# Attention scores on the two halves of TensorE: two of four query tiles with their halves swapped, and GpSimd's three steps on q and k in another order

## The chip, the cores and the metric

The kernel runs on one core of a Trainium2 chip. The metric is the device time of one execution in microseconds, the median of several runs. All work is in float32, on the core's five engines: TensorE (PE in the profile; PEld is its weight load), VectorE (DVE), ScalarE (ACT), GpSimd (POOL) and SyncE (SP), which issues the DMAs.

## The reference, cut to what matters

Four layers, each `x = x + layernorm(layer(layernorm(x)))`, on x of 2 batches x 512 tokens x 256 features. Only the first, causal attention with rotary positions, is touched by the change:

```python
q = rope((x @ wq.T + bq).reshape(b, s, 16, 128))
k = rope((x @ wk.T + bk).reshape(b, s, 16, 128))
v = (x @ wv.T + bv).reshape(b, s, 16, 128)
attn = einsum('bihd,bjhd->bhij', q, k) / sqrt(128)
attn = softmax(where(j > i, -inf, attn), axis=-1)
return einsum('bhij,bjhd->bihd', attn, v).reshape(b, s, 2048) @ wo.T + bo + residual
```

with `rope(x) = x * cos + rotate_half(x) * sin`. The other three are a feed-forward layer whose weights are unpacked from 4-bit codes (hidden size 2048, GELU), a linear attention with running sums, and a feed-forward layer whose weights are looked up in a table of 16 values (hidden size 688, SiLU).

## The kernel before, in words

**Tiles and halves.** A token tile is P = 128 tokens, so a batch has NT = 4 of them; HALF is 64. Once `halved[0]` is set, `matmul` (line 280) issues each matmul of 128 output rows as two of 64: the first writes PSUM partitions 0 to 63, the second 64 to 127. In the profile such a matmul has the form 128*64, and the two run on different column halves of the array. The text calls them A and B. A float32 matmul stands in the profile as two passes, each with its own weight load.

**Slots.** Attention is a loop over 32 heads (16 for each of 2 batches). `slot(i)` writes, in program order for each engine:

- the scores of head i, for the query tiles in the order 3, 2, 0, 1. Tile `it` sees (it+1) x 128 keys. `score_matmul` gives each half only the keys that its 64 queries may see: half A stops 64 keys before half B, and the 64 columns that A leaves out are filled with zeros by a small bf16 matmul (line 937), so that VectorE reads no stale PSUM. Tiles 2 and 0 share a PSUM bank; tile 1 lies in a bank of the tag "t".
- `scores` on VectorE: scores plus a causal mask, into the SBUF tile `p`, with a running minimum of the negated result; `exps` on ScalarE: the exponentials and their sums.
- `project` for q, then for k, of head i+1: four matmuls of 512 columns (two halves x two chunks of 128 features), then the rotary product. For k, ScalarE makes `ra` (k plus bias), GpSimd multiplies it by cosines; for q, VectorE makes bias, sum and product in one operation. VectorE makes two operations `rr` for the rotated part by sines. GpSimd adds `ra` and `rr` to qT or kT (for k of heads 0 and 1 VectorE does). In GpSimd's queue this stands as: q's sum, k's product by cosines, k's sum.
- the output projection of head i-2 (`projected_out`), accumulated over the heads of a batch in two PSUM banks; `attended` for head i-1 (probabilities by values: for key tile jt the 512 - 128 jt queries that see it); the transposed probabilities of head i (`turned_p`: VectorE's block transposes, then four DMAs to pT); one quarter of v for the group two ahead (`values`).

Head i+1's first score matmul needs qT and kT whole. Between the steps a slot also issues work for later layers: `dequantised` unpacks 4-bit weights (every second slot), `look_up` writes terms of a table look-up (VectorE makes a term, GpSimd adds it), and `vector.fill` puts steps of a selection wherever a planner in the file (`Times`, `Engine`, `now`, `until`, `poll`) expects VectorE to be free. The planner decides only the order of the program; nothing of it runs on the chip.

**Around it.** After the heads of a batch `after_attention` runs `norms` for units 0 and 1, or 2 and 3 (a unit is two token tiles); its last step is `yield until(to)`, which holds the chain back, in the planner's time, until its DMAs have landed. The first feed-forward layer begins inside the last slots (`next(main)`).

Of the kernel before, what the change touches and what calls it, by code (L numbers as in the profile page):

```python
# [10 lines left out]
F32 = mybir.dt.float32  # L11
I32 = mybir.dt.int32
# [7 lines left out]
P = 128  # L20
# [19 lines left out]
EPS = 1e-5  # L40
EPS_LIN = 1e-9
NEG = -1e30
WARM = 9
REST = INTER - (NO - 1) * P

# [144 lines left out]
def sandwich_kernel(  # L190
# [100 lines left out]
    def until(*aps):  # L291

        return max(0.0, times.written(*aps) - now[0])
# [30 lines left out]
    ident = const.tile([P, P], F32, name="ident")  # L324
    make_identity(nc, ident)

    mask = const.tile([P, S], F32, name="mask")

    def half(t, u):

        return t[:, HT * (u % 2) : HT * (u % 2) + HT, :]
# [26 lines left out]
    def norms(u, y, stage, to, eps=EPS, strided=False):  # L358

        x = [xs[u][:, j, :] for j in range(HT)]
        first = [stats(t, eps) for t in y]
        second = []
        for j in range(HT):
            yield until(first[j][0])
            add_scaled(x[j], y[j], first[j][0])
            second.append(stats(x[j], EPS))
        n = acts.tile([P, HT, D], F32, tag="ln", name=f"ln{stage}_{u}")


        by_blocks = (u, stage) != (NUNIT - 1, 3)
        for j in range(HT):
            rstd, shift = second[j]
            yield until(rstd, shift)
            to_n, from_x = n[:, j, :], x[j]
            if not by_blocks:
                to_n = to_n.rearrange("p (k f c) -> p k f c", k=NK, c=4)
                from_x = from_x.rearrange(
                    "p (c f k) -> p k f c" if strided else "p (k c f) -> p k f c", k=NK, c=4  # L380
                )
            elif strided:
                to_n = to_n.rearrange("p (k m) -> p k m", k=NK)
                from_x = from_x.rearrange("p (m k) -> p k m", k=NK)
            scalar.activation(to_n, from_x, AF.Identity, bias=shift, scale=rstd)
        yield until(n)
        if by_blocks:

            tr = acts.tile([P, 4, NK, HT, 32], F32, tag="ln", name=f"tr{stage}_{u}")
            for j in range(HT):  # L390
                vector.transpose(
                    tr[:, :, :, j, :], n[:, j, :].rearrange("p (k c f) -> p c k f", k=NK, c=4)
                )
            for a in range(4):
                sync.dma_start(
                    out=to[:, a].rearrange("p k j t -> p (k j t)"),
                    in_=tr[32 * a : 32 * a + 32].rearrange("f c k j t -> f c (k j t)"),
                )
        else:

            halved[0] = False
            pt = bank("t")
            for kc in range(NK):
                for j in range(HT):
                    transpose(
                        pt[:, kc * TU + j * P : kc * TU + (j + 1) * P],
                        n[:, j, kc * P : (kc + 1) * P],
                    )
            for kc in range(NK):
                scalar.copy(  # L410
                    to[:, :, kc].rearrange("p a j t -> p j a t"),
                    pt[:, kc * TU : (kc + 1) * TU].rearrange("p (j a t) -> p j a t", j=HT, a=4),
                )
        for j in range(HT):
            scalar.activation(x[j], x[j], AF.Identity, bias=first[j][1])
        yield until(to)


    terms = deque()
# [90 lines left out]
    with ExitStack() as at:  # L510
# [43 lines left out]
        def warm_up(n):  # L554
# [9 lines left out]
        xT0 = [  # L564
            ac.tile([P, NK, S] if b == 0 else [P, 4, NK, NT, 32], F32, name=f"xT0_{b}") for b in range(B)
        ]
        acc = ac.tile([P, NT, D], F32, name="h")


# [185 lines left out]
        def dequantised(packed, scales, u, name, w):  # L755
# [20 lines left out]
                    )  # L776
            p8 = dq.tile([P, UNIT], U8, tag="p8", name="p8")
            c8 = dq.tile([P, 2, UNIT], U8, tag="c8", name="c8")
            t8 = dq.tile([P, UNIT], U8, tag="t8", name="t8")
            two, t = p8.bitcast(I32), t8.bitcast(I32)  # L780
            low, high = c8[:, 0, :].bitcast(I32), c8[:, 1, :].bitcast(I32)

            def bits():
# [54 lines left out]

        def projection(kind, i, tag="mm"):

            b, h = divmod(i, NH)
            gg, hh = divmod(i, HG)
            w = wts[kind, gg]
# [6 lines left out]
            for cs in [slice(0, TU), slice(TU, S)] if i == 0 else [slice(0, S)]:  # L850
# [27 lines left out]
                )  # L878
                if first_half:
                    by_scalar()  # L880
            if (kind, i) == ("k", 1):
                inverted(0)
            (pool if i > 1 or kind == "q" else vector).tensor_add(to, a, r)
# [2 lines left out]
        def values(gg, pair, tag="mm"):  # L886
# [15 lines left out]
                    )  # L902
            scalar.copy(vs[gg][:, 2 * pair : 2 * pair + 2, :].rearrange("p t d -> p (t d)"), ps)

        def scores(i, it, ps):

            p, mn = ps_p[i]
            n = (it + 1) * P
            vector.tensor_tensor_reduce(
                out=p[:, p_at[it] : p_at[it] + n],  # L910
                in0=ps,
                in1=mask[:, S - n :],
                scale=-scale,
                scalar=3e38,
                op0=ALU.add,
                op1=ALU.min,
                accum_out=mn[:, it : it + 1],
            )


        zeros = mask[:, : HALF // 2].bitcast(mybir.dt.bfloat16)

        def score_matmul(i, it, ps):


            for q0 in (0, HALF):
                n = it * P + q0 + HALF
                matmul(
                    ps[q0 : q0 + HALF, :n],
                    qT[i][:, n - HALF : n],  # L930
                    kT[i][:, :n],
                    True,
                    True,
                    beside=q0 == 0,
                )
                if q0 == 0:
                    nc.tensor.matmul(  # L937
                        ps[:HALF, n : n + HALF], lhsT=zeros, rhs=zeros, start=True, stop=True
                    )

        def exps(i, it):
            p, mn = ps_p[i]
# [43 lines left out]
        def projected_out(i):  # L986

            b, h = divmod(i, NH)
            gg, hh = divmod(i, HG)
            if h == 0:  # L990
                yb[b] = [bank("o") for _ in range(NT // 2)]
            for t in range(NT):

                matmul(
                    yb[b][t // 2][:, (t % 2) * D : (t % 2 + 1) * D],
                    oT[i][:, t * P : (t + 1) * P],
                    wts["o", gg][:, hh, :],
                    h == 0 and t % 2 == 0,
                    h == NH - 1,
                    skip_group_check=True,  # L1000
                )

        def attention_sums(b):
            for t2 in range(NT // 2):
# [70 lines left out]
        def slot(i):  # L1075
# [29 lines left out]
            if now_in:  # L1105
                ps_p[i] = (
                    pr.tile([P, 1280], F32, tag="p", name="p"),
                    small.tile([P, NT], F32, tag="mn", name="mn"),
                )
                sums[i] = small.tile([P, NT], F32, tag="sm", name="sm")  # L1110
                s3 = bank("s")
                score_matmul(i, 3, s3)
                scores(i, 3, s3)
                s2 = bank("s")
                score_matmul(i, 2, s2[:, :384])
                score_matmul(i, 0, s2[:, 384:])
                scores(i, 2, s2[:, :384])
                exps(i, 3)
                scores(i, 0, s2[:, 384:])
                s1 = bank("t")  # L1120
                score_matmul(i, 1, s1[:, :256])
                scores(i, 1, s1[:, :256])
                exps(i, 2)
                exps(i, 0)
                exps(i, 1)
            catch_up()
            if i < NS - 2:
                look_up(i > 0)
            else:
                assert not terms  # L1130
            for kind in "qk":
                if kind == "q" and i in (0, 2, 3):
                    pass
                elif i + 1 < NS:
                    project(kind, i + 1)
                elif i <= NS:
                    next(main)
                    next(main)
                if kind == "q" and jobs and i % 2 == 0 and i >= 2:
                    dequantised(*jobs.popleft())  # L1140
                if kind == "q" and i and now_in:
                    inverted(i)
            if now_in:
                p, _ = ps_p[i]
                for it in reversed(range(NT)):
                    pi = p[:, p_at[it] : p_at[it] + (it + 1) * P]
                    scalar.mul(pi, pi, rs[i][:, it : it + 1])
# [14 lines left out]
            if now_in:  # L1162
                turned_p(i)
            if i in (1, 2):
                next(ahead, None)
            poll()
            if i < NS - HG:
                if i > 1:
# [9 lines left out]
        pair = projection("q", 0), projection("k", 0, "o")  # L1178
        next(pair[0])
        begin(first, next(first))  # L1180
        pool.affine_select(
            out=mask,
            in_=mask,
            compare_op=ALU.is_ge,
            fill=NEG,
            base=S - P,
            pattern=[[-1, S]],
            channel_multiplier=1,
        )
        halved[0] = True  # L1190
        next(pair[1])
        for step in (*pair, *pair):
            next(step, None)
        values(0, 0, "t")
        project("q", 1, "o")
# [318 lines left out]
```

## Time and profile before

| | |
|---|---|
| median of 3 runs | 626.18 us (626.04 to 626.4) |
| the profiled execution | 626.09 us, of which the span from the first to the last instruction is 624.3 us |
| TensorE | 617.4 us busy (99%), 4998 matmul records; granted clock 0.998 |
| VectorE | 487.9 us busy (78%) |
| ScalarE, GpSimd | 299.8 us (48%), 277.9 us (45%) |
| attention's slots | from 14.6 us to about 370 us |

A row of the profile's groups reads: line, engine, operation, output tile <- input tiles, shape, count, then busy time, mean ns of one and idle time ahead of it. A timeline row begins with its start and its length in us. A matmul's length runs to the modelled end of its pipeline, so that one begins before the end of the one ahead of it on the same half.

### The profile page before, as it was taken

Reading aid. Unit: us, or ns where it says so; the run is one execution under the profiler, and the core shown is the slowest. Engines: PE = TensorE matmul, PEld = TensorE weight load, DVE = VectorE, ACT = ScalarE, POOL = GpSimd, SP = SyncE. Lnnn points to the kernel's source line nnn. Section 1 sums busy time; section 2 is a strip of 40 time slices with the busy share of each in tenths; the row PEclk is TensorE's granted clock in tenths of the full one; section 3 lists DMA queues with packets and bytes.
Section 4 is the critical chain, followed back from the end, with each engine's and each line's share of the span. In section 5 each row is a group of like instructions: output and inputs, shape, how many; then the busy total and the mean of one; then the engine's idle time right before and its main releaser. Section 6 shows DMA issues by size and latency. Waiting matters only on the chain.

```text
span 624.3 us, 13250 instructions
## 1 busy us (share of the span) xinstructions
PE 617.4 (99%) x4998; PEld 443.5 (71%) x4998; DVE 487.9 (78%) x1159; ACT 299.8 (48%) x659; POOL 277.9 (45%) x351
## 2 busy tenths in 40 slices
PE   8999999999999999999999999999999999999996
PEld 6667766666676675677677789999766666666676
DVE  6979989877987989999998988779985372384853
ACT  5646666566565556656555751232213404416130
POOL 5355657355453465675667400450260151163341
PEclk9999999999999999999999999999999999999999
DMA  7467474575546646557462421311001001001000
GB/s 227 134 166 210 104 198 123 132 203 137 148 139 166 167 113 178 161 121 190 108 153 60 102 53 56 104 36 32 1 10 26 1 3 35 1 2 35 27 27 17
DMA packets 43600, 60.90 MB, mean 98 GB/s; under 512 B 5137, under 2 KB 31505, under 8 KB 43537
## 3 DMA queue, kind: packets, MB, share of 16 engines
q1 hardware_dynamic: 43536, 60.07, 36.9%
q8 instruction: 39, 0.64, 0.4%
q14 instruction: 25, 0.20, 0.1%
HBM read 28.33 MB, written 1.05 MB: 47 GB/s over the span
## 4 chain that ended last, share of the span: by engine, by line
PE 98%; issue 0%; DVE 0%; DMA 0%; POOL 0%; ACT 0%; POOLq 0%
PE ps_mm L280 40%; PE ps_o L280 22%; PE ps_s L280 21%; PE ps_t L280 15%; DMA x<-in_x 0%; DVE st L182 0%; PE ps_s L937 0%; POOLq L1510 0%; PE ps_t L287 0%; DVE mv L182 0%; POOL rstd L182 0%; ACT xT L182 0%; DVE x L182 0%; PE ps_s L287 0%; ACT wu L182 0%
## 5 line engine op out<-in xcount | busy, mean ns | idle before, releaser
L182 DVE SCALAR_TENSOR_TENSOR rr<-ps_mm,cols_sb,sin_sb 64x512 f32<-64x512 f32 (+1 forms) x126 | 93.4, 741 | 3.6 <-PE ps_mm L280 0.8
L182 POOL TENSOR_TENSOR wg<-wg,scratch 128x752 f32<-128x752 f32 x30 | 53.9, 1797 | 90.1 <-DVE scratch L182 87.4
L280 PE MATMUL ps_t<-pT,v 128*64 128x128 f32 (+3 forms) x512 | 88.6, 433 | 0.0
L280 PE MATMUL ps_mm<-xT,wg 128*64 128x256 f32 (+2 forms) x680 | 88.0, 379 | 0.0
L280 PE MATMUL ps_s<-xT,wu 128*64 128x256 f32 (+1 forms) x652 | 84.1, 379 | 0.0
L182 ACT ACTIVATE p<-p,mn 128x512 f32<-128x512 f32 (+3 forms) x128 | 70.6, 553 | 27.4 <-DVE mn L182 27.2
L280 PE MATMUL ps_o<-wd,hT 128*64 128x256 f32 (+2 forms) x676 | 78.4, 375 | 0.0
L280 PEld LDWEIGHTS ps_t<-pT,v 128*64 128x64 f32 x512 | 58.9, 137 | 23.8 <-issue 7.4
L280 PE MATMUL ps_o<-wo,oT 128*64 128x256 f32 x512 | 75.3, 379 | 0.0
L280 PE MATMUL ps_mm<-xT,wq 128*64 128x512 f32 (+2 forms) x252 | 73.9, 587 | 0.4 <-ACT xT L182 0.4
L280 PE MATMUL ps_mm<-xT,wk 128*64 128x512 f32 x248 | 73.2, 592 | 0.0
L280 PEld LDWEIGHTS ps_mm<-xT,wg 128*64 128x64 f32 (+2 forms) x680 | 59.5, 139 | 17.3 <-ACT ge L182 0.3
L280 PE MATMUL ps_s<-kT,qT 128*64 128x320 f32 (+5 forms) x384 | 71.5, 431 | 0.0
L280 PEld LDWEIGHTS ps_o<-wd,hT 128*64 128x64 f32 (+1 forms) x676 | 56.6, 141 | 19.6
L280 PEld LDWEIGHTS ps_s<-xT,wu 128*64 128x64 f32 (+1 forms) x652 | 57.6, 139 | 16.3 <-DVE hT L182 0.3
L280 PE MATMUL ps_mm<-wv,xTv 128*64 128x256 f32 x464 | 68.3, 379 | 0.0
L280 PEld LDWEIGHTS ps_o<-wo,oT 128*64 128x64 f32 x512 | 53.0, 137 | 19.9 <-issue 6.9
L182 ACT ACTIVATE p<-p,rs 128x512 f32<-128x512 f32 (+3 forms) x128 | 61.5, 551 | 10.1 <-DVE rs L182 8.2
L182 DVE CUSTOM_DVE_ANT_0 p<-ps_s,mask 128x512 f32<-128x512 f32 (+2 forms) x96 | 45.9, 509 | 25.6 <-PE ps_s L280 25.4
L182 POOL TENSOR_TENSOR qT<-ra,rr 128x512 f32<-128x512 f32 x32 | 40.9, 1277 | 47.9 <-DVE rr L182 47.9
L182 DVE STREAM_TRANSPOSE turned<-p 128x512 f32<-128x512 f32 (+3 forms) x128 | 54.1, 480 | 2.0 <-ACT p L182 1.1
L182 DVE TENSOR_TENSOR hT<-ge,ps_s 128x512 f32<-128x512 f32 x32 | 21.8, 683 | 41.4 <-ACT ge L182 22.9
(150 smaller groups left out, 992.5 us busy)
## 6 DMA issues: line engine op xcount, KB each, us to landing
pT<-turned SPq DMA_DIRECT2D x128, 208.0 KB, 3.9
wo<-in_wo SPq DMA_DIRECT2D x17, 256.0 KB, 4.0
wv<-in_wv SPq DMA_DIRECT2D x16, 256.0 KB, 4.0
wq<-in_wq SPq DMA_DIRECT2D x15, 256.0 KB, 4.7
wk<-in_wk SPq DMA_DIRECT2D x15, 256.0 KB, 4.5
xT<-tr SPq DMA_DIRECT2D x44, 64.0 KB, 2.2
pk_g<-in_gate_p SPq DMA_DIRECT2D x4, 256.0 KB, 4.2
sc_g<-in_gate_s SPq DMA_DIRECT2D x8, 128.0 KB, 4.1
```

What stands on the lines that cost most here:

```text
L182: return write(*args, **more)
L280: nc.tensor.matmul(out[part], lhsT=lhsT[:, part], rhs=rhs, start=start, stop=stop, **more)
```

## The change

1. `SWAPPED = (1, 2)`: in query tiles 1 and 2, the later 64 queries go to half A and the earlier 64 to half B. `score_matmul` becomes `score_half(i, it, late, ps)`, which issues one half of one tile, and `no_scores`, the zero fill. The order of issue becomes 3 early (A), 3 late (B), fill (A); 2 late (A), 2 early (B), 0 early (A), 0 late (B); 1 late (A), fill (B), 1 early (B). Tiles 2 and 0 lie in their shared bank so that each covers what the other leaves out, and need no fill.
2. The rows of `p` and the columns of pT and oT then stand in swapped order for tiles 1 and 2. `projected_out` puts them back: for each tile it issues the two halves itself, and sends each to the half where its tokens belong. In tiles 1 and 2 it issues B ahead of A.
3. The mask gets 128 columns more (the triangle for swapped tiles), moves to another SBUF pool, and is made by three selections of 128 columns instead of one of 512. `scores` reads it, the PSUM bank and `p` as blocks of 128 (64 for tile 0).
4. `projection` yields once more ahead of its sum. A slot first writes everything else of q and of k, and then the two sums. GpSimd's queue becomes: k's product by cosines, q's sum, k's sum. The dequantisation and the reciprocal `inverted(i)`, which stand between, are written ahead of both sums.
5. `dequantised` has no scratch tile `t8` of its own; it uses the first quarter of `pk`, the codes that it has read.
6. `norms` of unit 2 after attention ends with `yield 0.0` in the place of `yield until(to)`.

```diff
+SWAPPED = (1, 2)
-    mask = const.tile([P, S], F32, name="mask")
-        yield until(to)
+        yield 0.0 if (u, stage) == (2, 1) else until(to)
+        mask = ac.tile([P, S + P], F32, name="mask")
-            t8 = dq.tile([P, UNIT], U8, tag="t8", name="t8")
-            two, t = p8.bitcast(I32), t8.bitcast(I32)
+            two, t = p8.bitcast(I32), pk[:, : UNIT // 4]
...
+            yield
             if (kind, i) == ("k", 1):
                 inverted(0)
             (pool if i > 1 or kind == "q" else vector).tensor_add(to, a, r)
...
+        def score_half(i, it, late, ps):
+            n = it * P + (1 + late) * HALF
+            at = HALF * (late ^ (it in SWAPPED))
+            matmul(
+                ps[at : at + HALF],
+                qT[i][:, n - HALF : n],
+                blocks(kT[i][:, :n], HALF),
+                True,
+                True,
+                beside=not late,
+            )
...
+        def no_scores(ps):
+            nc.tensor.matmul(ps, lhsT=zeros, rhs=zeros, start=True, stop=True)
...
+                for half_ in range(2):
+                    at = HALF * (half_ ^ (t in SWAPPED))
+                    matmul(
+                        yb[b][t // 2][at : at + HALF, (t % 2) * D : (t % 2 + 1) * D],
+                        oT[i][:, t * P + half_ * HALF : t * P + (half_ + 1) * HALF],
+                        wts["o", gg][:, hh, :],
...
-                score_matmul(i, 3, s3)
-                scores(i, 3, s3)
+                score_half(i, 3, 0, blocks(s3[:, : S - HALF], HALF))
+                score_half(i, 3, 1, blocks(s3, HALF))
+                no_scores(s3[:HALF, S - HALF :])
+                scores(i, 3, blocks(s3, P))
                 s2 = bank("s")
-                score_matmul(i, 2, s2[:, :384])
-                score_matmul(i, 0, s2[:, 384:])
+                ps2 = s2[:, HALF : HALF + 3 * P]
+                ps0 = blocks(s2, P)[:, 0:4:3, :HALF]
+                score_half(i, 2, 1, blocks(ps2, HALF))
+                score_half(i, 2, 0, blocks(ps2[:, : 2 * P + HALF], HALF))
+                score_half(i, 0, 0, ps0[:, :1])
+                score_half(i, 0, 1, ps0)
...
-                score_matmul(i, 1, s1[:, :256])
-                scores(i, 1, s1[:, :256])
+                score_half(i, 1, 1, blocks(s1[:, :TU], HALF))
+                no_scores(s1[HALF:, TU - HALF : TU])
+                score_half(i, 1, 0, blocks(s1[:, : TU - HALF], HALF))
+                scores(i, 1, blocks(s1[:, :TU], P))
...
+            turning = []
             for kind in "qk":
...
-                    project(kind, i + 1)
+                    turning.append(projection(kind, i + 1))
+                    next(turning[-1])
+                    next(turning[-1])
...
+            for work in turning:
+                next(work, None)
```

More of the change, by code (lines that the diff above doesn't have):

```diff
@@ L903, in values, with blocks @@
             scalar.copy(vs[gg][:, 2 * pair : 2 * pair + 2, :].rearrange("p t d -> p (t d)"), ps)
+        def blocks(t, n):
+            return t.rearrange("p (b c) -> p b c", c=n)
         def scores(i, it, ps):
             p, mn = ps_p[i]
-            n = (it + 1) * P
+            n = HALF if it == 0 else P
+            masks = blocks(mask, P)
+            masks = (
+                blocks(mask[:, S - P : S], n),
+                masks[:, 0 : NT + 1 : NT],
+                masks[:, 0 : NT + 1 : NT // 2],
+                masks[:, :NT],
+            )
             vector.tensor_tensor_reduce(
-                out=p[:, p_at[it] : p_at[it] + n],
+                out=blocks(p[:, p_at[it] : p_at[it] + (it + 1) * P], n),
                 in0=ps,
-                in1=mask[:, S - n :],
+                in1=masks[it],
                 scale=-scale,
@@ L918, in scores @@
             )
-        zeros = mask[:, : HALF // 2].bitcast(mybir.dt.bfloat16)
[L923 to L939, printed above, removed]
+        def score_half(i, it, late, ps):
[8 more added lines that the diff above has]
+                beside=not late,
+            )
+        zeros = mask[:, : HALF // 2].bitcast(mybir.dt.bfloat16)
+        def no_scores(ps):
+            nc.tensor.matmul(ps, lhsT=zeros, rhs=zeros, start=True, stop=True)
         def exps(i, it):
@@ L992, in projected_out @@
             for t in range(NT):
[L994 to L1001, printed above, removed]
+                for half_ in range(2):
[4 more added lines that the diff above has]
+                        wts["o", gg][:, hh, :],
+                        h == 0 and t % 2 == 0,
+                        h == NH - 1,
+                        beside=half_ == 0,
+                        skip_group_check=True,
+                    )
         def attention_sums(b):
@@ L1111, in slot @@
                 s3 = bank("s")
-                score_matmul(i, 3, s3)
-                scores(i, 3, s3)
+                score_half(i, 3, 0, blocks(s3[:, : S - HALF], HALF))
+                score_half(i, 3, 1, blocks(s3, HALF))
+                no_scores(s3[:HALF, S - HALF :])
+                scores(i, 3, blocks(s3, P))
                 s2 = bank("s")
-                score_matmul(i, 2, s2[:, :384])
-                score_matmul(i, 0, s2[:, 384:])
-                scores(i, 2, s2[:, :384])
+                ps2 = s2[:, HALF : HALF + 3 * P]
[4 more added lines that the diff above has]
+                score_half(i, 0, 1, ps0)
+                scores(i, 2, blocks(ps2, P))
                 exps(i, 3)
-                scores(i, 0, s2[:, 384:])
+                scores(i, 0, ps0)
                 s1 = bank("t")
-                score_matmul(i, 1, s1[:, :256])
-                scores(i, 1, s1[:, :256])
+                score_half(i, 1, 1, blocks(s1[:, :TU], HALF))
+                no_scores(s1[HALF:, TU - HALF : TU])
+                score_half(i, 1, 0, blocks(s1[:, : TU - HALF], HALF))
+                scores(i, 1, blocks(s1[:, :TU], P))
                 exps(i, 2)
@@ L1164, in slot @@
             if i in (1, 2):
-                next(ahead, None)
+                for _ in ahead:
+                    pass
             poll()
@@ L1180, in sandwich_kernel @@
         begin(first, next(first))
[L1181 to L1189, printed above, removed]
+        for rows, cs, base in (
+            (slice(0, P), slice(S - P, S), 0),
+            (slice(0, HALF), slice(S, S + P), HALF),
+            (slice(HALF, P), slice(S, S + P), 0),
+        ):
+            pool.affine_select(
+                out=mask[rows, cs],
+                in_=mask[rows, cs],
+                compare_op=ALU.is_ge,
+                fill=NEG,
+                base=base,
+                pattern=[[-1, P]],
+                channel_multiplier=1,
+            )
         halved[0] = True
         next(pair[1])
-        for step in (*pair, *pair):
+        for step in (*pair, *pair, *pair):
             next(step, None)
```

## The prediction

> **What bounds the kernel now.** I read the page's shares of busy time first, then the groups of instructions with shapes apart, then the timeline of one head on TensorE and on GpSimd, and last the busy times by stretch.
>
> ```profile
> PE 617.4 (99%) x4998; PEld 443.5 (71%) x4998; DVE 487.9 (78%) x1159; ACT 299.8 (48%) x659; POOL 277.9 (45%) x351
> PE 98%; issue 0%; DVE 0%; DMA 0%; POOL 0%; ACT 0%; POOLq 0%
> ```
>
> TensorE is the bound, and at full clock. But "PE" is two halves here: each matmul of 128 output rows is written as two of 64, one for each half of the array's columns (A: PSUM rows 0 to 63, B: rows 64 to 127). The question is which half has the more to do. From the groups, TensorE's rows by shape:
>
> ```profile
> L280 PE MATMUL ps_mm<-xT,wk 128*64 128x512 f32 x248 | 73.2, 592 | 0.0
> L280 PE MATMUL ps_s<-kT,qT 128*64 128x384 f32 x64 | 25.9, 487 | 0.0
> L280 PE MATMUL ps_s<-kT,qT 128*64 128x320 f32 x64 | 23.4, 448 | 0.0
> L280 PE MATMUL ps_t<-kT,qT 128*64 128x256 f32 x64 | 19.0, 379 | 0.0
> L280 PE MATMUL ps_t<-kT,qT 128*64 128x192 f32 x64 | 16.6, 341 | 0.0
> L280 PE MATMUL ps_s<-kT,qT 128*64 128x128 f32 x64 | 12.2, 273 | 0.0
> L937 PE MATMUL ps_s<-mask 128*64 128x64 bf16 x96 | 17.9, 193 | 0.0
> ```
>
> Each score shape stands 64 times for 32 heads: a float32 matmul is two passes. The means rise by 213 ns from 256 to 512 columns and by 106 ns from 128 to 256: **0.832 ns a column** and some 166 ns of latency that overlaps the next pass. The zero fill of 64 bf16 columns streams for 193 - 166 = 27 ns. The shapes that follow a fill are too long: 320 columns should mean 166 + 266 = 432 and mean 448, 192 should mean 326 and mean 341. That is 31 ns on the first of two passes, so a fill costs its half some 59 ns.
>
> Now one head (a "slot"), columns for each half: q, k, v and the output projection 1024 each, probabilities by values 1280. Scores: A 448 + 320 + 64 + 192 = 1024 and four fills; B 512 + 384 + 128 + 256 = 1280. B has 6656 columns: x 2 passes x 0.832 = 11.08 us. A has 6400: 10.65 us and 0.24 of fills. The timeline confirms it:
>
> ```profile
> 199.42 1.34 PE L280 MATMUL ps_s<-kT,qT 128*64 128x512 f32 x5
> ...
> 200.92 0.27 PE L280 MATMUL ps_s<-kT,qT 128*64 128x128 f32 x1
> 200.93 0.64 PE L280 MATMUL ps_mm<-xT,wq 128*64 128x512 f32 x1
> 201.03 0.27 PE L280 MATMUL ps_s<-kT,qT 128*64 128x128 f32 x1
> 201.14 0.59 PE L280 MATMUL ps_t<-kT,qT 128*64 128x256 f32 x2
> ...
> 210.31 0.59 PE L280 MATMUL ps_s<-kT,qT 128*64 128x448 f32 x1
> 210.40 0.38 PE L280 MATMUL ps_mm<-wv,xTv 128*64 128x256 f32 x1
> 210.61 1.02 PE L280 MATMUL ps_s<-kT,qT 128*64 128x512 f32 x3
> ```
>
> The 512-column scores are B's. They start at 199.42 and 210.61, so a slot takes 11.19 us: B's 11.08 and 2 ns for each of 52 passes. B has no gap. At 200.93 A is already in the next q projection while B has the 128 and 256 to do. At 210.31 A's 448 starts, although A's last 256-column pass, by its order in the list, began some 0.5 us before and streams for 0.21: A waits, B doesn't.
>
> **What the Trainium skill says.** "TensorEngine Tiling (Array Packing)", Key Properties: tiles execute weight loads and matmuls in parallel. The trace agrees: the two halves overlap throughout. "TensorE: Matmul & The Clock Gate", Part 3, What overlaps and what doesn't: matmuls start and end in program order. The trace differs: the q projection of 200.93 stands in the program behind the 256 of 201.14. The measurement decides; the halves drift apart. The same page, Part 1, gives a fixed 2.5 ns a matmul; here it is (11.19 - 11.08) / 52 = 2 ns.
>
> **The change, part by part.** *Scores.* With tiles 1 and 2 swapped, A gets 448 + 384 + 64 + 256 = 1152, B 512 + 320 + 128 + 192 = 1152. Two fills go; A keeps one, B gets one. B: 128 columns x 2 x 0.832 = 213 ns less, 59 ns more: **154 ns less a slot**. A: 213 more, three fills (177) less: 36 more. Scores then take 1152 x 1.664 + 59 + 20 = 2.00 us on either half, against 2.15 on B.
>
> *Output projection.* The same eight matmuls, now in the order AB BA BA AB. It costs nothing if a half can pass a pair of the other that is still waiting, as A did above.
>
> *kT, which the next scores wait for.* A's lead was A's cover: now neither half has one, so A's wait counts in full. GpSimd in this slot:
>
> ```profile
> 206.39 1.28 POOL L182 TENSOR_TENSOR qT<-ra,rr 128x512 f32<-128x512 f32 x1 [7.74 <-DVE rr L182]
> 207.62 1.29 POOL L182 TENSOR_TENSOR ra<-ra,cos_sb 128x512 f32<-128x512 f32 x1
> 208.98 1.27 POOL L182 TENSOR_TENSOR kT<-ra,rr 128x512 f32<-128x512 f32 x1
> ```
>
> kT ends at 210.25 and A's 448 starts 0.06 later; B comes 0.30 later still. New order: k's product, q's sum, k's sum. The product waits for ScalarE's k (205.27 + 0.69 = 205.95, some 0.15 earlier in the shorter slot, since it follows TensorE). It starts near 205.9, and three operations of 1.28 with 0.1 between end at 209.85. q's sum waits behind the product, but its input (VectorE, 206.24) is there, as is k's (207.99). The scores would be due at 210.61 - 0.15 = 210.46: 0.6 to spare (0.15 in the old order). In the other slots, where VectorE is not late, kT ended 0.75 before B; the new chain begins with ScalarE there too, ends some 0.15 earlier in step with TensorE, and keeps 0.6. So the move is worth nothing by itself on the clock of before, and insures the first part. On VectorE, ScalarE and SyncE nothing is passed but the reciprocal and a dequantisation's loads, which do not feed k or q.
>
> *VectorE.* Four mask operations a slot now walk blocks of 128 or 64. No row shows that; I take 0, with bounds of -0.05 and +0.3 us a slot. Cover:
>
> ```profile
> 199.42:210.61 11.19, 11.19 (x86) 8.33 (x84) 9.76 (x25) 6.71 (x16) 3.79 (x3) 1.00 0.54 135
> 210.61:221.81 11.19, 11.19 (x87) 6.72 (x85) 10.87 (x27) 6.17 (x15) 6.17 (x6) 1.00 0.62 171
> ```
>
> VectorE has 1.4 us idle in the first stretch and 0.3 in the second, one of the fullest (another, from 233.0 us, has 10.95 busy). 11.04 still holds both, with kT's 0.6 to absorb a late slot.
>
> *First slot.* From 14.60 to 22.00 VectorE sets the end: it adds kT itself, until 21.84, behind a full queue, and TensorE starts within 0.15 of it. The shorter scores bring nothing there.
>
> *The rest, each at 0.* The mask: 640 columns to clear for 512 (0.52 becomes about 0.65, done near 2.1 us, GpSimd idle until 3.8); three selections of 128 columns (0.29 each by the identity's row) for one of 0.63: 0.25 more near 10 us, before a qT that ends 0.8 ahead of kT. The dequantisation's scratch in pk: the next load of pk comes a slot after its last use. The wait left out after unit 2's norms: unit 3's statistics are issued some us earlier, on VectorE with 29.3 of 120 us idle (380 to 500), while TensorE is busy for 120.00 of 120.00; bounds -0.1 and +0.3.
>
> **Sum.** 31 slots x 0.154 = 4.77 us; taken 4.7 for a small wait in the special slots 2 to 4. The profiled execution took 626.09 us (span 624.3, 1.8 around it), 0.09 under the median of 626.18. 626.1 - 4.7 = 621.4; by the median 621.5. I write **621.4**.
>
> **Rivals.**
> - *The halves are not free of each other* (slower). If program order holds more strictly in the new sequences than in those seen, a half waits out a pair wherever one half comes twice running: 2 x 0.215 = 0.43 us a slot in the output projection. 32 x 0.43 - 4.8 = +9: 635. It decides from 0.154 us of such stalls a slot. For it: the page's sentence, and A did stop now and then for lack of room to run ahead (its q pass of 200.93 is 0.64 long and not 0.59). Against: A passed three waiting passes of B there; with no lead, fewer have to be passed. 5%.
> - *VectorE takes over.* With +0.3 us a slot, the ten fullest slots lose their gain and some others part: 2 to 3 us left, 623.5. For it: 10.95 of 11.19 busy; against: 10.0 in the mean of the slots that I looked at. 13%.
> - *kT is late* because GpSimd holds q's sum for a late ScalarE. It takes 0.6 us to be felt and 0.75 to cost the gain: 626. 3%.
> - *The change doesn't do what it says*, A and B sharing one stream: no time in it but two fills, 626. A's own wait at 210.31 speaks against it. 3%.
>
> **How the numbers follow.** The forecast, 620.6 to 622.3, has 76%. The range takes VectorE's case in: 620.5 to 623.7. A difference of 0.2% (1.25 us) is about what a measurement of this kernel can tell from none. Faster 0.90 (forecast, VectorE's case, and a little of the others), same 0.05, slower 0.05.
>
> **What would show it.** From one slot's first 512-column score to the next: 11.04 us. Fills: 64 and not 128. Score shapes of 512, 448, 384, 320, 256, 192, 128 and 64 as before, but the 512 and the 448 begin within 0.1 us of each other and the next q projection begins on both halves at once. GpSimd's kT ends 0.5 us or more before the scores. From 400 us on nothing changes but the clock time. I am wrong if slots stay at 11.19, if gaps stand in the output projection, or if scores start right behind a kT.

## The result, and the profile after

| | before | after |
|---|---|---|
| median | 626.16 us (626.04 to 626.47) | 622.16 us (621.99 to 622.6) |
| profiled execution | 626.09 us, span 624.3 | 622.14 us, span 620.0 |
| slot, from one head's first 512-column score to the next | 11.19 us | 11.04 us |
| first score to the last output projection | 376.04 us | 371.44 us |
| from there to the end of the last matmul | 228.75 us | 228.95 us |

The ratio is 0.9936 [0.9923, 0.9949]: 4.0 us faster. 621.4 was predicted. The page of the kernel after, its busy line and its chain:

```profile
PE 613.4 (99%) x4938; PEld 433.8 (70%) x4938; DVE 484.1 (78%) x1159; ACT 299.6 (48%) x659; POOL 275.5 (44%) x353
PE 98%; DVE 1%; issue 0%; DMA 0%; POOL 0%; ACT 0%; POOLq 0%; DVEq 0%
```

The bound is still TensorE, with less to do. The groups with shapes apart (count, busy us, mean ns):

```profile
L281 PE MATMUL ps_s<-kT,qT 128*64 128x384 f32 x64 | 26.9, 501 | 0.1
L281 PE MATMUL ps_s<-kT,qT 128*64 128x320 f32 x64 | 22.5, 433 | 0.0
L951 PE MATMUL ps_t<-mask 128*64 128x64 bf16 x32 | 6.2, 193 | 0.0
L951 PE MATMUL ps_s<-mask 128*64 128x64 bf16 x32 | 6.2, 192 | 0.0
```

Fills are 64 and not 128. The 320-column score, now without a fill ahead of it, has come down from 448 to 433 ns, and the 384, which now follows one, has gone up from 487 to 501: 14 ns in the mean of two passes, so the gap of some 30 ns after a fill moved with the fill. TensorE's timeline across a slot:

```profile
208.14 1.02 PE L281 MATMUL ps_s<-kT,qT 128*64 128x512 f32 x4
...
210.13 0.63 PE L281 MATMUL ps_mm<-xT,wq 128*64 128x512 f32 x2
...
219.17 1.02 PE L281 MATMUL ps_s<-kT,qT 128*64 128x512 f32 x4
...
221.17 0.64 PE L281 MATMUL ps_mm<-xT,wq 128*64 128x512 f32 x2
```

A row takes neighbouring passes of several shapes together. Here 448 and 512 start so close that they fall into one row of four passes; before, the 448 had a row of its own 0.30 us ahead. The scores last 1.99 us (208.14 to 210.13) on both halves, and the slot 219.17 - 208.14 = 11.03. GpSimd in the slot that ends at 208.14:

```profile
203.60 1.28 POOL L183 TENSOR_TENSOR ra<-ra,cos_sb 128x512 f32<-128x512 f32 x1 [7.30 <-ACT ra L183]
204.84 1.28 POOL L183 TENSOR_TENSOR qT<-ra,rr 128x512 f32<-128x512 f32 x1
206.08 1.28 POOL L183 TENSOR_TENSOR kT<-ra,rr 128x512 f32<-128x512 f32 x1
```

The chain begins with ScalarE's `ra` and ends at 207.36, 0.78 us before the scores. VectorE's mask operations, now in blocks, and two of its fullest slots by stretch (the columns: PE, PEld, DVE, ACT, POOL busy, clock, DMA):

```profile
L183 DVE CUSTOM_DVE_ANT_0 p<-ps_s,mask 128x512 f32<-128x512 f32 x32 | 22.0, 686 | 23.1 <-PE ps_s L951 23.1
L183 DVE CUSTOM_DVE_ANT_1 p<-ps_s,mask 128x384 f32<-128x384 f32 x32 | 17.8, 556 | 1.7 <-PE ps_s L281 0.4
```

```profile
208.14:219.17 11.03, 11.03 (x84) 6.78 (x82) 10.43 (x27) 6.17 (x15) 6.07 (x6) 1.00 0.65 174
318.52:329.56 11.04, 11.04 (x86) 8.17 (x84) 10.90 (x23) 6.66 (x16) 7.49 (x6) 1.00 0.43 101
```

686 and 556 ns (687 and 555 before; the two shorter ones are as before within 1 ns): blocks cost nothing here. A slot with VectorE 10.90 of 11.04 us busy still takes 11.04.

### The profile page after: what moved, and what is told of

It reads as the page before. It is cut to its first block, busy times and chain, and to the rows that moved or that the text cites. A ratio compares the mean times of both kernels' runs of the same rounds, so it can differ in the third digit from the quotient of the medians.

```text
span 620.0 us, 13144 instructions
## 1 busy us (share of the span) xinstructions
PE 613.4 (99%) x4938; PEld 433.8 (70%) x4938; DVE 484.1 (78%) x1159; ACT 299.6 (48%) x659; POOL 275.5 (44%) x353
## 4 chain that ended last, share of the span: by engine, by line
PE 98%; DVE 1%; issue 0%; DMA 0%; POOL 0%; ACT 0%; POOLq 0%; DVEq 0%
PE ps_mm L281 40%; PE ps_o L281 22%; PE ps_s L281 21%; PE ps_t L281 15%; DMA x<-in_x 0%; DVE st L183 0%; PE ps_t L288 0%; DVE hT L183 0%; POOLq L1546 0%; POOL rstd L183 0%; DVE mv L183 0%; ACT xT L183 0%; DVE x L183 0%; PE ps_s L288 0%; ACT wu L183 0%
## 5 line engine op out<-in xcount | busy, mean ns | idle before, releaser
L281 PE MATMUL ps_t<-pT,v 128*64 128x256 f32 (+3 forms) x512 | 75.5, 433 | 0.0
L281 PEld LDWEIGHTS ps_t<-pT,v 128*64 128x64 f32 x512 | 45.4, 137 | 31.3 <-issue 22.6
L281 PE MATMUL ps_o<-wo,oT 128*64 128x256 f32 x512 | 61.8, 379 | 0.0
L281 PE MATMUL ps_mm<-xT,wq 128*64 128x512 f32 (+2 forms) x252 | 59.8, 583 | 0.4 <-ACT xT L183 0.4
L183 POOL TENSOR_TENSOR ra<-ra,cos_sb 128x512 f32<-128x512 f32 (+1 forms) x33 | 41.0, 1244 | 41.7 <-ACT ra L183 39.1
L281 PE MATMUL ps_mm<-xT,wk 128*64 128x512 f32 x248 | 59.5, 592 | 0.0
L281 PE MATMUL ps_s<-kT,qT 128*64 128x384 f32 (+5 forms) x384 | 57.7, 427 | 0.1
L281 PE MATMUL ps_mm<-wv,xTv 128*64 128x256 f32 x464 | 56.0, 379 | 0.0
L183 ACT ACTIVATE ln<-x,shift,rstd 128x256 f32<-128x256 f32 x24 | 14.9, 626 | 76.7 <-POOL shift L183 76.7
L183 DVE CUSTOM_DVE_ANT_0 p<-ps_s,mask 128x512 f32<-128x512 f32 x64 | 31.1, 486 | 23.1 <-PE ps_s L951 23.1
```

What stands on the lines that cost most here:

```text
L183: return write(*args, **more)
L281: nc.tensor.matmul(out[part], lhsT=lhsT[:, part], rhs=rhs, start=start, stop=stop, **more)
```

## The experiments

"Spare" is the time from the end of GpSimd's (in head 1, VectorE's) kT to the first 512-column score that needs it; 0.06 us means that TensorE started right behind it. Slots are counted from 0. TensorE's time is read as two stretches: "attention", from the first score to the end of the last output projection, and "behind", from there to the end of the last matmul. Attention differs by some 0.3 us between profiles whose regular slots agree, mostly in the lengths of slots 2 and 3. Each ratio is against the kernel before as it ran beside the experiment, with medians from 626.34 to 626.65 us.

**1. The swap alone.**

```diff
-            yield
             if (kind, i) == ("k", 1):
...
-                    turning.append(projection(kind, i + 1))
-                    next(turning[-1])
-                    next(turning[-1])
+                    project(kind, i + 1)
...
-        yield 0.0 if (u, stage) == (2, 1) else until(to)
+        yield until(to)
```

> The kernel after, with GpSimd's old order (q's sum, k's product, k's sum) and with the old wait in norms put back; the halves stay swapped (the scratch in pk stays too, since the longer mask leaves no room for t8). Theory H (a slot lasts as long as the half with more columns: 2 passes x 0.832 ns a column, plus 59 ns a fill on that half): slots of 11.04 us, about 622.2 us as with the whole change; kT ends some 0.2 us ahead of the scores in the slots where VectorE is late, instead of 0.7 to 0.8, so still no wait. Theory K (the earlier kT is what brought the time): no gain, 626 us.

626.16 us against 626.65, ratio 0.9994 [0.9988, 1.0001]: **nothing is gained**, where 622.2 was expected. Yet attention is 371.70 us, 4.3 less than before, with slots of 11.04. Spare was 0.31 us in every second slot from 5 to 19, where VectorE is late, and 0.70 to 0.83 in most others; kT was late in slot 20 alone (11.26, then 11.09). The gain is lost behind attention: 232.87 us against 228.75. There the chain that ended last no longer runs on TensorE alone. From it, between 443 and 459 us, the pieces of 0.6 us and more:

```profile
443.10 0.68 DVE hT L183
444.26 1.34 POOL k L183
445.62 2.33 DVE ks L183 x2
448.05 0.70 DVE den L183
449.20 0.61 DVE v L183
449.83 1.27 DVE kvs L183 x2
451.10 3.29 DVE den L183 x4
454.46 0.80 POOL lT L183
455.31 4.11 PE ps_o L281 x36
```

and VectorE's longest wait in that stretch (total, times, longest):

```profile
DVE st L183 <- PE ps_o L281: 6.3, 1, 6.3
```

VectorE stands 6.28 us, up to 407.20, ahead of a statistic (`st`) of an output that TensorE has not made. Its selection steps, which it writes in program order behind that, come late, and with them the linear attention's sums. Nothing of what runs there was edited: the planner wrote another order, because the swap had changed what it expects. By the traces, TensorE and GpSimd have the order of the kernel after there, while VectorE's and ScalarE's is one that neither before nor after has. That this wait is the whole of the 4 us is not shown; that the 4 us lie behind attention is.

**2. GpSimd's order alone**, in the kernel before.

```diff
+            yield
...
-                    project(kind, i + 1)
+                    turning.append(projection(kind, i + 1))
+                    next(turning[-1])
+                    next(turning[-1])
...
+            for work in turning:
+                next(work, None)
```

> The kernel before, with GpSimd's new order alone (k's product, q's sum, k's sum). Theory H: half B stays at 6656 columns, slots of 11.19 us, 626.2 us within 0.2; half A's wait of 0.29 us ahead of its 448 columns in every second slot goes, and A's lead over B grows in its place until A stops elsewhere. Theory K: 622 us.

626.47 against 626.65, ratio 0.9998 [0.9989, 1.0006]; attention 375.99, behind 228.78. Without the swap the order is worth nothing.

**3. After, with the wait back**, and **4. after, with GpSimd's old order back.** These fill the table between 1 and the change.

```diff
-        yield 0.0 if (u, stage) == (2, 1) else until(to)
+        yield until(to)
```

> After, with the wait at the end of unit 2's norms put back. Which of the two small parts keeps the stretch behind attention (210.7 us from the last output projection to the last transposes in the profile after, 214.6 in the kernel that has neither GpSimd's new order nor the wait left out)? Theory O (GpSimd's order, through the planner's course): the wait doesn't matter, the stretch stays at 210.7 and the time at 622.2. Theory Y (the wait left out): the stretch goes to 214.6 and the time to 626. With the instructions of every engine in the order of after, as they are in this program, I expect O's number here: 622.2.

Experiment 4 is experiment 1 without the last hunk of its diff:

> After, with GpSimd's old order (q's sum, k's product, k's sum) and nothing else put back; that is, the swap alone plus the wait left out. Attention stays at 371.7 us as in the swap alone. Behind it: theory O says 214.6 us up to the last transposes, so 626; theory Y, that the wait left out is what mends that stretch, 210.7 and 622.4. A third: each of the two changes the course, and either is enough; then it is Y's number here and O's with the wait put back.

| swap | GpSimd's order | unit 2's wait | attention | behind | median |
|---|---|---|---|---|---|
| no | old | kept (before) | 376.04 | 228.75 | 626.16 |
| no | new | kept | 375.99 | 228.78 | 626.47 |
| yes | old | kept | 371.70 | 232.87 | 626.16 |
| yes | old | left out | 371.75 | 228.78 | 622.14 |
| yes | new | kept | 371.37 | 229.03 | 622.19 |
| yes | new | left out (after) | 371.44 | 228.95 | 622.16 |

With the swap, either of the two small parts is enough, and without both the 4 us go. Ratios of the two new rows: both 0.9931 [0.9919, 0.9944]. With the wait back, the traces show the instructions of after in the same order on TensorE, VectorE, ScalarE and GpSimd. With the old order and the wait left out, ScalarE and GpSimd run behind attention in the order of before, and VectorE nearly so. So the two parts don't add up: each leads the planner, on its own, to an order that works. On the clock of attention the old order costs little: kT is late in slots 20 and 23 (11.26, 11.09, then 11.19, 11.09), 0.47 us in this profile.

**5. One tile swapped instead of two.**

```diff
-SWAPPED = (1, 2)
+SWAPPED = (2,)
```

(with tile 1's mask, order and fill as before)

> The kernel after with tile 2 alone swapped: scores A 448 + 384 + 64 + 192 = 1088 columns and two fills, B 512 + 320 + 128 + 256 = 1216 and none. Theory H: B sets the slot, 6592 x 1.664 + 0.11 = 11.08 us, half way: 626.2 - 31 x 0.107 = 622.9, plus the 0.5 us that the kernel after loses outside its slots, 623.4 us. Theory I (the gain is that of 64 fills fewer, whichever half had them): the fills are as few as after, so 622.2 us.

623.33, ratio 0.9944 [0.9931, 0.9956]. Slots of 11.09: B has 64 columns less than before, 64 x 2 x 0.832 = 106 ns, 11.19 - 0.11 = 11.09. The slot follows the longer half's columns at both points; the fills are as few as after, so their number is not what brings the gain.

**6. and 7. One fill more on A**, right behind the first one, in the kernel before and after.

```diff
+                no_scores(s3[:HALF, S - HALF :])
```

> The kernel before with one zero fill more a slot on half A (the same 64 columns of tile 3 once again). Theory H: A has 0.24 us a slot to spare, nothing: 626.2 us within 0.2. Theory I (every fill costs its 0.06 us, whichever half has it): 32 x 0.06 = 1.9 more, 628.1 us.

> The kernel after with the same fill more on half A. Theory H: A has nothing to spare now; 32 x 0.057 = 1.8 us more, 624.0 us, with B ahead of A by a growing lead. A fill that costs nothing here, as in the kernel before, would speak against halves that are both full.

Before: 626.81 against 626.53, ratio 1.0004 [0.9996, 1.0013]. All regular slots stay at 11.19. Its profile's attention is 0.8 us longer, nearly all of it in slot 3 (10.25 for 9.48), through a transfer:

```profile
PE ps_t L280 <- DMA pT<-turned: 0.6, 1, 0.6
```

After: 623.14, ratio 0.9944 [0.9929, 0.9958]; slots of 11.07 to 11.08 from the sixth on, 33 to 36 ns longer each, attention 0.87 longer. So half A had room before and has none after, as the columns say. The second fill costs 33 to 36 ns and not the 59 that a fill on its own costs. In the trace it begins 29 ns behind the first, and the 384-column score behind it still means 501 ns, as with one fill: two fills in a row share the gap of 31 ns behind them, so one more adds its 27 ns of streaming and little else. The expected size was wrong by that gap.

**8. and 9. kT made later**, by a sum of 128 or of 384 columns written ahead of kT's own on GpSimd.

```diff
+            if kind == "k" and i > 1:
+                pool.tensor_add(to[:, :384], a[:, :384], r[:, :384])
```

> The kernel after with a sum of k's first 128 columns on GpSimd ahead of k's whole sum (done twice, same values), which makes kT some 0.45 us later. Theory H: the traces of after show 0.65 to 0.85 us between kT and the scores, so nothing: 622.2 us within 0.3. If kT's end ruled the time, 28 slots x 0.45 = 12 us more.

> The same with 384 columns, some 1.0 us later: more than the spare time. Theory H: each of 28 slots waits for what the delay has over 0.65 to 0.85, less the 0.06 from kT to the scores: 0.2 to 0.4 us a slot, 6 to 11 us in all, 628 to 633 us; both halves then start their scores together behind kT.

The short one: 623.98, ratio 0.9956 [0.9941, 0.9971], more than the expected 622.2 within 0.3. From slot 4 to slot 29 all but five stay at 11.04, with 0.21 to 0.29 us to spare at the end of nearly all of these. What it costs, 1.5 us of attention, lies in slot 3 (10.49 for 9.41; there the whole sum itself stands at 2.20 us instead of 1.28, and no view here says why) and in slots 20 and 24 (0.20 and 0.15, and 0.05 in the slot after each and in slot 4). The long one: 635.84, ratio 1.0144 [1.0127, 1.0161], slower. Its GpSimd and TensorE:

```profile
201.99 2.35 POOL L183 TENSOR_TENSOR kT<-ra,rr 128x384 f32<-128x384 f32 x2
```

```profile
204.39 1.08 PE L281 MATMUL ps_s<-kT,qT 128*64 128x448 f32 x4
```

```profile
PEld ps_s L281 <- POOL kT L183: 20.1, 28, 2.0
```

The two sums end at 204.34 and the scores start at 204.39, 0.05 later: kT now sets every slot. The added sum is 2.35 - 1.28 = 1.07 us long, most slots are 11.40 to 11.43, 0.38 longer: 1.07 - 0.38 = 0.69 us is what was spare. The spare time is real, over half of it is what the new order bought in the slots where VectorE is late, and without it both halves wait. The total is above the expected 628 to 633: slot 3 takes 1.6 us more than after, slots 20 and 24 take 0.9 each and slots 26 to 29 from 0.45 to 0.7; why these take more than the others is not shown.

**10. The output projection with A always first.**

```diff
-                for half_ in range(2):
-                    at = HALF * (half_ ^ (t in SWAPPED))
+                for at in (0, HALF):
+                    half_ = (at // HALF) ^ (t in SWAPPED)
```

> The kernel after with the output projection's halves always issued A, B in each tile (the same matmuls to the same places), so that no half comes twice running there. Theory H: a half passes the other's waiting pair, the order costs nothing, 622.2 us within 0.15. Theory S (program order holds a half back where one half comes twice): faster, by up to 0.4 us a slot; some 0.1 to 0.3 us in all would be seen if S holds only where the halves have drifted apart.

621.91 us, ratio 0.9924 [0.9911, 0.9936], slots of 11.04 (but for slot 20, 11.20): the order AB BA BA AB costs nothing, so no half waits out a pair of the other.

**11. More work for VectorE.**

```diff
-            vector.tensor_tensor_reduce(
+            for engine in (vector, nc.vector) if it == 0 else (vector,):
+              engine.tensor_tensor_reduce(
```

> After, with tile 0's mask operation on VectorE written twice in each slot: 0.29 us more (its own row) and a short one on its minimum, outside of what the planner knows, so that all other instructions stay in their order. This is about the upper bound (+0.3 us a slot) that the prediction set for the mask operations in blocks. The prediction's own price for that case: ten full slots lose their gain and some others part, 2 to 3 us in all, so 624.2 to 625.2. The rival: kT's spare of 0.75 us in nearly every slot takes the longer VectorE chain up, a full slot's rest goes over into the next one, and what is left is under 1 us, seen in slot 20, 23 and 24 alone: 622.2 to 623.0.

623.06, ratio 0.9942 [0.9929, 0.9956]: 0.9 us lost by the medians and 1.1 in attention by the profiles, not 2 to 3. The added row, and by stretch the first slot and one of the fullest:

```profile
L923 DVE CUSTOM_DVE_ANT_0 p<-ps_s,mask 128x128 f32<-128x128 f32 x32 | 9.3, 292 | 1.1
```

```profile
14.53:22.27 7.74, 7.38 (x62) 4.66 (x60) 6.45 (x17) 3.68 (x11) 2.56 (x2) 1.00 0.54 181
208.35:219.39 11.04, 11.04 (x86) 7.68 (x82) 10.80 (x29) 6.17 (x15) 5.89 (x6) 1.00 0.65 174
```

The first slot takes the whole of the 0.29 and a little more (7.40 before, 7.74 here), since VectorE sets its end. The full slot takes none: VectorE is 10.80 of 11.04 busy (the slot that was 10.90 busy stays at 11.04 too), and kT's spare time shrinks to 0.5 to 0.6 in the slots where VectorE is late (0.11 once, and 0.06, none, at the end of slot 3). The rest of the loss is 0.47 in slot 26, where TensorE waits for a pT transfer, 0.27 from the last slot on, and 0.05 in slot 4. The slots named in the expectation were the wrong ones; the size was about right (at most 623.0 was expected).

**12. The last transposes later.**

```diff
-        yield until(n)
+        yield until(n) + (0.0 if by_blocks else 0.9)
```

> After, with the last layer's transposes (but for those of the first unit's own kind) written 0.9 us of the planner's time later, so that four more matmuls stand ahead of them on TensorE. In the profile after, TensorE stands 0.22 us there for ScalarE's ln. Theory: the wait goes, nothing else moves, 622.16 - 0.22 = 621.9, attention unchanged at 371.4. Rival: what hangs on the transposes is pushed back by the four matmuls, 4 x 0.22 = 0.9 us, and the end comes up to 0.7 later: 622.9.

The transposes of the last layer in the kernel before, in the kernel after, with the wait in them, and with this edit, from TensorE's timelines:

```profile
600.52 0.66 PE L287 MATMUL ps_t<-ident,ln 128*128 128x128 f32 x4
```

```profile
596.83 0.88 PE L288 MATMUL ps_t<-ident,ln 128*128 128x128 f32 x4
```

```profile
597.82 0.65 PE L288 MATMUL ps_t<-ident,ln 128*128 128x128 f32 x4
```

0.88 becomes 0.65, and the stretch behind attention 228.75 us, what it was before the change. 621.74 us (621.57 to 622.4), ratio 0.9925 [0.9912, 0.9939]: the lowest median of all the kernels here. Of the 0.4 us between this and after, 0.2 is the stretch behind attention and some 0.2 lies outside the span (1.74 to 1.83 us in these five runs, 1.99 to 2.14 in the six of after). So it beats before for certain; that it beats after is not shown, since the intervals overlap and experiment 10, without this edit, has a ratio as low.

## Why the prediction was right, point by point

- **The bound and the slot: right.** B's columns set the slot, 154 ns fewer make 11.04, and 11.04 it is in all but a few slots. Experiments 5, 6 and 7 show the rule at four points: what is added to the shorter half is free, what is added to the longer one, or to either when they are level, counts.
- **"2 ns for each of 52 passes": a miscount that cost nothing.** By the profile's counts a half makes 40 float32 passes in a slot (8 each of scores, output projection, values and probabilities by values, 4 each of q and k), so what stands over the columns is (11.19 - 11.08) / 40 = 2.8 ns a pass, a little above the figure that the prediction compares it with and not below it. The sum carries the 0.11 us as measured, so the forecast doesn't change.
- **A fill at 59 ns: right where it stands alone**, as the two shapes that changed by 14 ns and the slots, 0.15 us shorter, show; wrong for a second one behind it (33 to 36 ns).
- **The output projection at nothing: right.** Its sixteen passes take 1.72 us of the timeline after (213.57 to 215.29), eight of 0.215 on each half and no gap, and the rival that half a pair is waited out is gone with experiment 10.
- **kT's spare 0.6 us in the new order: right**, a little low (0.65 to 0.84 in regular slots from the fourth on; 0.69 by experiment 9). In the old order 0.15 was predicted: 0.3 in the slots where VectorE is late, and 0.06, none, in one slot of experiment 1 and two of experiment 4.
- **VectorE: mask operations at 0, right to a nanosecond.** The rival that VectorE takes over was priced too high: with 0.29 us more a slot, about 1 us goes and not 2 to 3. The failed step is "the ten fullest slots lose their gain": a full slot's surplus goes into kT's spare time.
- **The first slot bringing nothing: right**, 7.40 before and after.
- **"31 slots x 0.154 = 4.77; taken 4.7": 4.60 measured.** From the first score to the last slot's first score, 30 slots, the gain is 4.61; slot 3 gives 0.07, and slot 21 gives 0.05 more than its share, since a small wait of before goes. The last slot gives nothing: in both kernels its scores wait for VectorE's `hT` (0.9 us before). From the waits of TensorE's weight loads in the kernel after, 350 to 390 us:

```profile
PEld ps_s L281 <- DVE hT L183: 0.5, 1, 0.5
```

- **The rest, "each at 0": this is the term that was mis-sized**, and with it "From 400 us on nothing changes but the clock time". Behind attention VectorE, ScalarE and TensorE run in another order than before, and the stretch is 0.20 us longer (228.95 for 228.75). TensorE's transposes come earlier in its order than ScalarE's ln is ready, 0.88 us for 0.66 before; experiment 12 puts them later and the 0.20 are back. The wait left out, for which the prediction kept its bounds, is not the cause: the 0.20 stand with the wait back too (229.03) and are absent with GpSimd's old order (228.78). Besides, the profiled execution has 2.2 us outside its span and not 1.8, and starts its scores 0.07 later; the start differs by more than that between the profiles here. The account: 626.09 - 4.60 + 0.20 + 0.07 + 0.4 = 622.16, against 622.14. Of the 0.8 us between prediction and measurement (622.16 - 621.4), 0.1 is the sum of slots, 0.2 the transposes, the rest start and end, of which no experiment shows the cause.
- **"So the move is worth nothing by itself on the clock of before, and insures the first part": right for attention, and missed what it does elsewhere.** The prediction priced GpSimd's order and the wait left out each alone, on the instructions that they touch. Through the planner they decide how the program behind attention is written. With the swap and neither of them, 3.9 us of the gain would have been lost (232.87 for 228.95 behind attention) in code that no line of the diff touches. That the change as a whole avoids this was luck as far as the prediction goes: its sum for attention rests on a mechanism that the experiments bear out, but that nothing would be lost behind attention it took without a reason that holds.

## What to carry to other kernels

Where TensorE's columns are split in two halves, count the columns for each half: here the slot followed the longer one, and moving columns to the shorter one paid, less the fill that came with it, until they were level. From then on the work that feeds both (here kT) needs spare time of its own, since the half that used to run ahead no longer covers it. Where a program's order comes from a planner in the source, compare the program order of a change away from the edit as well as at it, and test small parts together: a part that is worth nothing alone can be what keeps the gain of another.

## What the runs showed of the hardware that was not expected

- A second zero fill directly behind the first costs 33 to 36 ns of its half and not 59: the gap of some 30 ns stands before the float32 matmul that follows, once.
- The time outside the span is about as large an uncertainty as the small terms of the sum, and it goes in part with the program: 1.99 to 2.14 us in the six runs of after, 1.73 to 1.86 in the 21 of experiment 1, 1.74 to 1.83 in the five of experiment 12. What sets it is not shown.
